# A written order for the last routing group of a mixture-of-experts layer, woven with pieces of expert work already known

## The chip, the cores and the metric

The kernel runs on one core of one Trainium2 chip. The core has a matrix engine (PE, with its weight load shown apart as PEld), a vector engine (DVE), a scalar engine (ACT), GpSimd (POOL) and SyncE (SP). Each executes its own instructions in the order in which they stand; they meet through semaphores. Transfers are issued from the queues of SP, ACT and POOL. The metric is the device time of one execution in microseconds. Lines such as L1087 are lines of the kernel before.

## The reference

The program computes four layers over 2708 rows of 256 values; only layer 1 is touched. It normalizes the rows, adds a graph product, normalizes again, and sends every row through one of eight experts:

```python
# graph part
A = adj + I;  d = 1/sqrt(A.sum(1));  A = A * d[:, None] * d[None, :]
x = x + relu(A @ (layernorm(x) @ W) + b)
# expert part: one expert for each row, all experts share the hidden layer
xf = layernorm(x)
H = gelu(xf @ W1 + b1)                    # 256 -> 1024
probs = softmax(H @ Wg + bg)              # 8 experts
assign = argmax(probs)
out = sum over e of where(assign == e, probs[:, e] * (H @ Wd[e] + bd[e]), 0)
x = x + out
```

## The kernel before

The 2708 rows are 22 tiles of 128, the last with 20 rows. Layer 1 works in three groups (`GROUPS1`): tiles 0 to 7, 8 to 15 and 16 to 21. For each group the graph sums are made by a loop over all blocks of the adjacency (L1174), into four banks `acc2`. When a group's sums are complete, `grow` on DVE takes them out of the banks and adds them to `x` (L1125, L1127): these are the sums' exits.

Then `send1` routes the group. `stats` makes means and variances and takes the reciprocal root by a Newton iteration on DVE. For each pair of tiles `norm_to` (L187) normalizes on DVE, `turn_to` transposes on PE (L203) and copies on ACT (L204); `hidden` makes the eight slices of the hidden layer on PE (L357) with a Gelu on ACT (L359); sixteen gate products (L1070), a copy on ACT (L1073) and a folding product (L1077) give the logits, to which DVE adds the bias (L1078). The hidden rows are turned by DVE's block transposes into `hrow`, of which there are two buffers (L1087), and stored to `hid` in the main memory, four transfers for a tile (L1093, L1096 for the last tile). In the first two groups GpSimd issues these stores; in the last one ACT does. After the last pair come a softmax (L327 to L334, its exponential needs another table on ACT, L135), the choice of the best expert, and `route`, which gives each row its place in its expert's list (L384, L386 and small operations on DVE). GpSimd scatters the rows' names and weights to these places, one transfer for each tile (`taken`, L492). `blocks` turns the experts' counts into a table that says for each block of 128 list places which expert it has and where its names lie.

`Units` does the experts' work in such blocks. For a block GpSimd gathers the names (L506) and then the rows of the hidden layer (L643, three buffers `hs`), SP fetches the expert's weights (`wb`, L1010, three buffers of 1152 KB), PE turns the rows by eight transposes (L654), ACT copies them (L655), PE makes sixteen products (L693), DVE adds the bias and applies the weight (L694, L695, two buffers `ys`), and GpSimd scatters the output rows to `given` (L492). Nine blocks are certain once two of the three groups are routed: they hold only rows of the first two groups. The next fifteen need the routing of the last group. A conditional region for still more blocks follows, and then layer 2.

What stands in a program is not the order on an engine: a planner with estimated costs orders the instructions of each engine by readiness and by their place in the program. Edges between two instructions (`after`, `add_manual_dep`) restrict it. In the kernel before, `send1` of the last group comes first in the program and the nine certain blocks with the fifteen others after it, in `work1.run(hc, items, beside)`, and the planner weaves them. The weaving shown in the timeline is its choice. `beside` is called by `run` for each block, and for block 13 (`NA + 4`) it adds work for layer 2: two loads of rows and one of weights by GpSimd, eight operations on DVE (L259, L260) and a centring product (L235, L237).

## Time and profile before

| what | us |
|---|---|
| median of three runs | 1936.62 (1930.79 to 1938.07) |
| the profiled execution | 1935.32 |
| its span, first to last instruction | 1933.6 |
| PE busy in the span | 1827.5 |
| last group's sums end, first exit begins | 930.1 |
| first transposes of the last group's pairs | 950.45 |
| last logit of the last group | 990.35 |
| softmax's sum | 996.32 |
| end of PE's work on certain blocks and the centring | 1012.2 |
| first transposes of an uncertain block | 1028.51 |
| last product of an uncertain block | 1101.25 |
| layer 2 begins to load | 1108.4 |

Times from 930 on are microseconds after the start of the span. A line of a stage's busy time gives the window, its length, the busy time and count of each engine, the mean granted clock of PE as a share of full speed, the share of the transfer engines that was busy and their rate. A line of the timeline gives start, duration, engine, line, operation, operands and count; in brackets stands how long the engine was idle before it and what ended that. SPq, ACTq and POOLq are issues of transfers.

### The profile page before, as it was taken

Reading aid. Unit: us, or ns where it says so; the run is one execution under the profiler, and the core shown is the slowest. Engines: PE = TensorE matmul, PEld = TensorE weight load, DVE = VectorE, ACT = ScalarE, POOL = GpSimd, SP = SyncE. Lnnn points to the kernel's source line nnn. Section 1 sums busy time; section 2 is a strip of 40 time slices with the busy share of each in tenths; the row PEclk is TensorE's granted clock in tenths of the full one; section 3 lists DMA queues with packets and bytes.
Section 4 is the critical chain, followed back from the end, with each engine's and each line's share of the span. In section 5 each row is a group of like instructions: output and inputs, shape, how many; then the busy total and the mean of one; then the engine's idle time right before and its main releaser. Section 6 shows DMA issues by size and latency. Waiting matters only on the chain.

```text
span 1933.6 us, 25684 instructions
## 1 busy us (share of the span) xinstructions
PE 1827.5 (95%) x9453; PEld 1327.0 (69%) x9453; DVE 1092.7 (57%) x2439; ACT 642.1 (33%) x1461; POOL 344.5 (18%) x405
## 2 busy tenths in 40 slices
PE   7999989999998999999796799999899999999998
PEld 6888778888887888888676678888557732232344
DVE  7776862444333524444441175555354398999897
ACT  7868732222223303122231142223232552031131
POOL 1005263333321002314336300000000000000000
PEclk9999989999998999999898999999899999999999
DMA  8435476887764454535777620000101000000000
GB/s 274 138 114 155 120 273 243 342 311 282 301 254 133 144 151 118 149 106 131 222 243 262 264 75 1 1 1 1 44 1 33 17 1 23 23 12 28 20 20 15
DMA packets 90141, 243.94 MB, mean 126 GB/s; under 512 B 18159, under 2 KB 44823, under 8 KB 80792
## 3 DMA queue, kind: packets, MB, share of 16 engines
q1 hardware_dynamic: 70048, 197.09, 30.9%
q0 software_dynamic: 16960, 42.42, 6.9%
q10 hardware_dynamic: 3000, 2.70, 0.5%
q8 instruction: 78, 1.28, 0.3%
q14 instruction: 55, 0.45, 0.1%
HBM read 216.29 MB, written 28.71 MB: 127 GB/s over the span
## 4 chain that ended last, share of the span: by engine, by line
PE 73%; DMA 12%; DVE 6%; issue 5%; ACT 2%; POOL 2%; SPq 0%; POOLq 0%; DVEq 0%; ACTq 0%
PE num L1803 10%; PE ps_acc L1382 9%; PE acc L1174 8%; PE ps_tmp L357 7%; PE acc L893 7%; PE den L1813 6%; PE ps_acc L591 5%; PE yacc L601 4%; PE ps_tmp L250 4%; DMA given<-ys,xs 4%; PE ps_acc L1566 3%; PE yacc L693 2%; DMA hs<-hid,names 2%; DMA given<-ys,names 1%; PE ps_tmp L203 1%
## 5 line engine op out<-in xcount | busy, mean ns | idle before, releaser
L1773 DVE SCALAR_TENSOR_TENSOR e<-arena,G,mask 128x1024 f32<-128x1024 f32 (+1 forms) x264 | 287.0, 1149 | 13.6 <-PE den L1813 13.6
L1803 PE MATMUL num<-e,wh 128*64 128x512 f32 (+4 forms) x1056 | 215.8, 551 | 0.0
L1382 PE MATMUL ps_acc<-hh,e 128*128 128x257 f32 x882 | 199.2, 382 | 1.7 <-ACT o L1327 1.7
L893 PE MATMUL acc<-msg,wt 128*128 128x256 f32 x882 | 198.5, 382 | 2.0 <-DVE wt L851 1.2
L1174 PE MATMUL acc<-sup,adrow 128*128 128x256 f32 x882 | 198.6, 382 | 1.8 <-DVE adrow L1146 1.8
L893 PEld LDWEIGHTS acc<-msg,wt 128*128 128x128 f32 x882 | 165.6, 191 | 28.0 <-DVE wt L851 2.1
L1174 PEld LDWEIGHTS acc<-sup,adrow 128*128 128x128 f32 x882 | 165.1, 190 | 28.7 <-issue 5.2
L1382 PEld LDWEIGHTS ps_acc<-hh,e 128*128 128x128 f32 x882 | 163.7, 190 | 29.2 <-ACT o L1327 4.3
L591 PE MATMUL ps_acc<-xTs,wa 128*128 128x256 f32 (+1 forms) x768 | 170.6, 375 | 1.0 <-DVE xTs L564 0.8
L593 ACT ACTIVATE hTs<-ps_acc,wa 128x256 f32<-128x256 f32 (+1 forms) x192 | 88.6, 464 | 244.4 <-PE yacc L601 165.6
L601 PE MATMUL yacc<-wb,hTs 128*128 128x256 f32 x736 | 167.4, 380 | 1.9 <-DVE ys L603 1.9
L591 PEld LDWEIGHTS ps_acc<-xTs,wa 128*128 128x128 f32 x768 | 137.6, 191 | 27.3 <-DVE xTs L564 3.8
L1803 PEld LDWEIGHTS num<-e,wh 128*64 128x64 f32 (+1 forms) x1056 | 66.5, 136 | 127.3 <-issue 106.5
L601 PEld LDWEIGHTS yacc<-wb,hTs 128*128 128x128 f32 x736 | 137.6, 190 | 20.2 <-DVE ys L603 2.7
L1376 DVE SCALAR_TENSOR_TENSOR e<-Rb,G,mask 128x640 f32<-128x640 f32 (+2 forms) x110 | 85.1, 775 | 93.1 <-PE ps_acc L1382 93.0
L1813 PE MATMUL den<-e,wh 128*32 128x512 f32 (+4 forms) x1056 | 118.0, 548 | 0.0
L204 ACT COPY xT<-ps_tmp 128x256 f32<-128x256 f32 x98 | 33.6, 364 | 242.5 <-PE ps_tmp L203 217.2
L1143 DVE TENSOR_SCALAR mask<-adrow 128x1024 uint8<-128x1024 f32 (+1 forms) x66 | 41.7, 631 | 124.2 <-DMA adrow<-in_adjT 124.0
L693 PE MATMUL yacc<-wb,hTs 128*128 128x256 f32 x384 | 90.6, 387 | 0.3 <-DMA wb<-in_L_ffn_Wdp 0.3
L851 DVE SCALAR_TENSOR_TENSOR wt<-adrow,wt 128x640 f32<-128x640 f32 (+3 forms) x67 | 71.1, 1063 | 30.6 <-ACT wt L141 30.3
L1813 PEld LDWEIGHTS den<-e,wh 128*32 128x32 f32 (+1 forms) x1056 | 30.2, 108 | 77.9 <-issue 73.8
L492 POOL DMA_INDIRECT given<-ys,xs x46 | 65.9, 1432 | 83.7 <-DVE ys L604 77.9
(452 smaller groups left out, 2570.8 us busy)
## 6 DMA issues: line engine op xcount, KB each, us to landing
adhalf<-in_adjT SPq DMA_DIRECT2D x42, 677.0 KB
wb<-in_L_ffn_W2p SPq DMA_DIRECT2D x24, 1152.0 KB
wb<-in_L_ffn_Wdp SPq DMA_DIRECT2D x24, 1152.0 KB
wa<-in_L_ffn_W1b SPq DMA_DIRECT2D x24, 1028.0 KB
adrow<-in_adjT SPq DMA_DIRECT2D x42, 512.0 KB
adrow<-in_adjT SPq DMA_DIRECT2D x42, 320.0 KB
adrow<-in_adjT SPq DMA_DIRECT2D x21, 576.0 KB
adrow<-in_adjT SPq DMA_DIRECT2D x21, 448.0 KB
```

What stands on the lines that cost most here:

```text
L357: te.matmul(p[:, :w], lhsT=w1[:, c, f * P : (f + 1) * P], rhs=xnT[:, c, c0 : c0 + w], start=(c == 0), stop=(c == DC - 1))
L591: te.matmul(p[:, f % 2, : m * P], lhsT=w1[:, c, f * P : (f + 1) * P], rhs=xT[:, c, : m * P], start=(c == 0), stop=(c == DC - 1))
L593: s.activation(hT[:, f, : m * P], p[:, f % 2, : m * P], AF.Gelu, bias=bias[:, f : f + 1])
L601: te.matmul(q[:, k, :], lhsT=hT[:, f, k * P : (k + 1) * P], rhs=w2[:, f, :], start=(f == 0), stop=(f == HC - 1))
L693: te.matmul(q, lhsT=hT[:, f, :], rhs=w2[:, f, :], start=(f == 0), stop=(f == HC - 1))
L893: te.matmul(p[:q, n - pair[0], :], lhsT=wt[:, k : k + q], rhs=msg[:r, j, :], start=(j == 0 and n == pair[0]), stop=(j == FULL - 1 and n == ...
L1174: te.matmul(p[:q, n - pair[0], :], lhsT=ad[:, k : k + q], rhs=sup[:r, j, :], start=(j == 0 and n == pair[0]), stop=(j == FULL - 1 and n == ...
L1376: v.scalar_tensor_tensor(e[:r, :w], Rb[:r, c0 : c0 + w], G[:r, j, :], mask[:r, j, c0 : c0 + w], op0=ALU.max, op1=ALU.mult)
L1382: te.matmul(p[:, : D + 1], lhsT=e[:, k : k + q], rhs=hh[:, j, :], start=(j == 0), stop=False)
L1773: v.scalar_tensor_tensor(e[:, :w], slow[:, m % 2, k, :w], G[:, j, 2 * pair + k, :], mask[:, j, c0 : c0 + w], op0=ALU.max, op1=ALU.mult)
L1803: te.matmul(num[k * DK : (k + 1) * DK, hf, :q], lhsT=wh[some, j, 2 * pair + k, :DK], rhs=e[some, h0 - c0 : h0 - c0 + q], start=(j == 0), s ...
L1813: te.matmul(den[z : z + Q, :q], lhsT=wh[some, i, 2 * pair + k, DK : DK + 1] .to_broadcast([some.stop - some.start, Q]), rhs=e[some, h0 - c ...
```

## The change

Only the last group of layer 1 is treated differently. `Units.run` becomes `add` (put blocks on the list) and `pieces`, a generator that gives control back after each block's transposes and after each block's output. `send1` is cut into parts (`normed`, `first_products`, `gate_products`, `add_up`, `keep`). For the last group it takes the generator as `fill` and calls for a piece at written places: the transposes of blocks 0, 1, 2 and 3 and the products and outputs of blocks 0 and 1 lie between the parts of the three pairs. The sums' exits are now bank by bank, each followed by the statistics of its own two tiles, and the first two norms follow the first statistics. At the end `in_order` chains every instruction made since the exits began on PE, DVE and ACT, transfers issued by ACT among them, to the one before it on its engine; it is the helper that stood further down, moved up. The last pair's hidden rows are stored after this and by GpSimd; the first two pairs' by ACT as before. The operations of `beside` on DVE get an edge behind the last output made so far, that of block 12.

```diff
+        def pieces(self, pool, during=None):
+
             turned = self.turn(pool, self.rows[0][1])
+            yield
             n = 0
             while self.rows:
                 w2, hT = self.ahead.pop(0), turned
...
                 if self.rows:
                     turned = self.turn(pool, self.rows[0][1])
+                    yield
                 y = pool.tile([P, D], F32, name="ys", bufs=2)
...
-                v.tensor_scalar(y, y, m[:, 1:2], None, op0=ALU.mult)
+                i = v.tensor_scalar(y, y, m[:, 1:2], None, op0=ALU.mult)
+                self.last = i.ins.name
                 scatter(self.given, m[:, 0:1].bitcast(I32), y, self.given.shape[0] - 1, self.ok)
+                yield
...
-                queue = s if tiles is GROUPS1[-1] else g
+            def keep(own, hT, queue):
...
+            if fill is None:
+                st = stats(tiles)
+                for own in pairs:
+                    hT = first_products(own, normed(own, (0, st)))
+                    add_up(own, gate_products(own, hT))
+                    keep(own, hT, g)
+            else:
+                start, st, made = begun
+                next(fill)
+                xT = normed(pairs[0], None, made)
+                for n, own in enumerate(pairs):
+                    hT = first_products(own, xT)
+                    next(fill)
+                    lT = gate_products(own, hT)
+                    if n + 1 < len(pairs):
+                        xT = normed(pairs[n + 1], (2 * (n + 1), st[n + 1]))
+                        next(fill)
+                    add_up(own, lT)
+                    if n + 1 < len(pairs):
+                        keep(own, hT, s)
+                in_order(start, (mybir.EngineType.PE, mybir.EngineType.DVE,
+                                 mybir.EngineType.Activation))
+                keep(own, hT, g)
             pin()
...
+        def beside(b):
+            if b == NA + 4:
+                first = len(nc.cur_bb.bb.instructions)
+                left.append(blocks_left(too_many, MOST))
...
+                centre(w_l2)
+                for i in nc.cur_bb.bb.instructions[first:]:
+                    if i.engine == mybir.EngineType.DVE:
+                        tc.add_manual_dep(i, work1.last, mybir.DependencyInfo(
+                            mybir.DependencyClass.NoSync, mybir.DependencyReason.DATA),
+                            reason="order")
...
+            else:
+                begun = len(nc.cur_bb.bb.instructions), [], []
+                for n in range(0, len(tiles), 2):
+                    grown(n // 2)
+                    begun[1].append(stats(tiles[n : n + 2]))
+                    if n == 0:
+                        for k in range(2):
+                            begun[2].append(work.tile([P, D], F32, name="xn"))
+                            norm_to(begun[2][k], tiles[k], k, begun[1][0])
                 sums.close()
                 gnn.close()
                 psum_pool(l1, 3, 3)
...
                 work1.more()
+                between = work1.pieces(hc, lambda b: beside(b))
+                send1(tiles, begun, between)
+                break
...
-        work1.run(hc, items, beside)
+        work1.add(items)
+        for _ in between:
+            pass
         work1.run_rest(hc, more, left[0])
```

The helper, moved up unchanged:

```python
    def in_order(first, engines):

        was = {}
        for i in nc.cur_bb.bb.instructions[first:]:
            if i.engine in engines:
                if i.engine in was:
                    tc.add_manual_dep(i, was[i.engine], ...)   # order only, no semaphore
                was[i.engine] = i.name
```

## The prediction

> **What bounds the kernel now.** I read the page's shares first, then the busy time by stage around the change, then the timeline of that stretch engine by engine, then the waits. The whole program sits on the matrix engine:
>
> ```profile
> span 1933.6 us, 25684 instructions
> PE 1827.5 (95%) x9453; PEld 1327.0 (69%) x9453; DVE 1092.7 (57%) x2439; ACT 642.1 (33%) x1461; POOL 344.5 (18%) x405
> ```
>
> PE is busy 95% of the span, so time can only come from PE's holes or from half clock. Busy time by stage (PE, PEld, DVE, ACT, POOL, then PEclk, DMA share, GB/s) shows one hole inside the stretch that the change rewrites:
>
> ```profile
> 931.00:943.00 12.00, 3.37 (x18) 2.43 (x16) 9.13 (x40) 2.24 (x4) 5.47 (x6) 0.73 0.94 345
> 943.00:990.00 47.00, 46.46 (x276) 38.78 (x276) 13.14 (x32) 18.80 (x42) 12.79 (x13) 0.96 0.74 250
> 1012.00:1028.50 16.50, 0.16 (x1) 0.02 (x1) 2.77 (x8) 0.00 (x0) 10.67 (x13) 0.59 0.88 244
> 1028.50:1101.30 72.80, 68.46 (x360) 58.89 (x360) 12.50 (x34) 17.48 (x31) 39.41 (x39) 0.98 0.80 295
> ```
>
> From 1012 to 1028.5 PE does nothing: the nine certain blocks are used up and the first uncertain block waits for its hidden rows. The timeline shows why that comes late (start, length, engine, line, operands, idle before):
>
> ```profile
> 949.65 0.42 DVE L694 TENSOR_TENSOR ys<-yacc,wb 128x256 f32<-128x256 f32 x1 [9.35 <-PE yacc L693]
> 949.99 1.87 DVE L187 TENSOR_SCALAR xn<-x,mv,rs_y 128x256 f32<-128x256 f32 x5
> ...
> 960.89 3.84 ACTq L1093 DMA_DIRECT2D hid<-hrow  x8
> ...
> 971.86 0.71 DVE L1087 STREAM_TRANSPOSE hrow<-hT 128x512 f32<-128x512 f32 x1 [3.58 <-DMA hid<-hrow]
> ...
> 990.20 0.15 DVE L1078 TENSOR_TENSOR lg<-ps_tmp,L_ffn_bg 20x8 f32<-20x8 f32 x1 [0.51 <-PE ps_tmp L1077]
> ...
> 991.27 2.46 ACTq L1096 DMA_DIRECT2D hid<-hrow  x4
> ...
> 993.76 1.28 ACT L135 ACT_TABLE_LOAD   x1 [4.72 <-DMA hid<-hrow]
> ...
> 996.32 0.20 DVE L332 TENSOR_REDUCE s_sm<-s_e 128x6 f32<-128x48 f32 x1
> ...
> 1019.17 0.42 DVE L694 TENSOR_TENSOR ys<-yacc,wb 128x256 f32<-128x256 f32 x1 [9.57 <-DMA given<-ys,names]
> ...
> 1028.51 1.94 PE L654 MATMUL ps_acc<-ident,hs 128*128 128x128 f32 x8 [16.35 <-DMA hs<-hid,names]
> ```
>
> Statistics are done at 940.3, but the first block's output (L694) stands ahead of the norms on DVE, so pair work starts at 950. The last logit is there at 990.35; then ACT is still issuing stores until 993.7, loads the exponential's table, and the softmax's sum runs at 996.32. From there to the first uncertain block 32.1 us pass: routing, six scatters, the names gather, the rows gather. That chain, not PE, sets 1028.5. I take it unchanged.
>
> **The change, part by part.** I lay out the new order with durations of this execution. One block is T (eight transposes, 0.87) and P (sixteen products, 3.46); these and PE's other lengths come from the pieces of the chain of waits between 950 and 992.
>
> *Start.* DVE's first sums' exit is at 930.08 as before. Two tiles' exits (0.88 + 0.75), four statistics operations (1.1), variance and eleven Newton operations spaced 0.2 as at 939.3 to 940.3 (2.35), two norms (0.75): the first norm is ready at 935.5 instead of 950.4. Eight operations on the next layer's weights (L259, L260, 0.4 each, 3.2 in sum), which lay among the statistics, go behind block 12's output. The other two pairs' exits and statistics follow on DVE until 945.3, beside the first pair's products; cover is thin, for pair two's norms (to 946.1) are wanted at 946.2.
>
> *Pair one.* PE transposes 0.9 and two copies on ACT, products from 936.9 for 6.9; the Gelu table (1.28) is nearly hidden by the three free banks, 0.3 left: 944.1. T of block 1, 945.0; gate 1.2, 946.2; pair two's transposes 947.1; P of block 0, 950.55; folding 0.4, 950.95.
>
> *Pair two: the price of writing the order.* DVE now does block 0's output (0.8), logits (0.35) and only then four transposes (2.6): 954.4. Before they ran as soon as half of the Gelus were done. Behind them ACT issues eight stores at 0.48 each (the row of 3.84), from 953.15 to 957.0, and the next Gelu stands behind those. PE fills its three banks (2.6) by 953.55, then stands for 4.0. After 4.9 us of idleness at 934.5 the next eight transposes took 1.94 instead of 1.04, and half clock lasted some 3.5 us after the restart at 1028.5 (granted clock 0.50 from 1027 to 1031, 0.86 from 1031 to 1035), so a stall costs another 1.75, bounds 0 and 1.8; I take 1.75. Products end 963.6; T 0.87, gate 1.2, transposes 0.7, P 3.46, folding 0.4: 970.3.
>
> *Pair three.* Three banks 1.6 (the 148-column products, 4.03 for eight), 971.8. DVE's output, logits and transposes end 973.7, ACT's stores 976.2, the stall is 4.9, and with half clock the products end 981.1. T 0.9, gate 0.9, copy and folding 0.8: last logit at 984.1, 6.2 before the old one. In sum the start gains 14.9 and the order gives back 8.7.
>
> *Last rows' stores.* ACT loses eight issues (989.0 to 993.7), so the table load can begin at once; from last logit to the softmax's sum were 6.0, and could be 1.0. Against this, pair three's DVE transposes wait until pair two's stores have landed (9.0 us from issue by the row at 971.86), that is until about 985, and they may stand ahead of the softmax. Bounds: gain 5.0, or 0 if an output of block 2 (PE 3.46) stands ahead too. I take 3.8, nearer the first: at 996.3 one output (0.8) stood ahead of that sum, and the transposes' wait for the stores adds about 1. GpSimd gains eight issues of 0.553 (its own row for the earlier groups), 4.4, between 979 and 990, before the six scatters can start near 992; queued behind them are rows gathers with two blocks of slack. Cost zero while routing covers it; 4.4 if it doesn't.
>
> The Trainium skill's page DMA: Bandwidth & Descriptors, section Issuing engine by pattern, speaks against this part: plain stores belong on the hardware-generated queues, which it calls generally faster. By that rule the 4.6 us on ACT would be the cheap place and this term no gain, 1929.6 in place of the sum below; the rows say that the place matters more than the issue, since nothing short of a table load waits behind ACT's.
>
> *Sum for the chain.* 6.2 + 3.8 = 10.0: the first uncertain block at 1018.5. PE's supply until then: at 983.9 seven P and five T remain, 28.6, and 2.0 of routing products, to 1014.5. So PE stands 4 us in place of 16.35, and the chain still sets the time.
>
> *After.* The centring of next layer's weights (PE 1.03, DVE 4) falls among the uncertain blocks, where PE waits for rows anyway; 0 to 3, taken 0.5. DMA share was 0.88 in the hole and would carry the same bytes in less time; the first five uncertain blocks ran at 4.22 each and the later ten at 5.17, so losing that head start could cost up to 4.8; taken 0, since their rows are asked for after the names in either order. SP's weight fetches wait for block outputs, as now. Gain 9.5 us.
>
> **The sum.** The profiled execution took 1935.3 (span 1933.6 and 1.7 around it), 1.3 under the median 1936.6. 1935.3 - 9.5 = 1925.8. Measurements of this kernel tell about 0.5%, 9.7 us.
>
> **Rivals.**
> - *No stalls.* If the planner's free instructions or quicker stores close both stalls, and half clock stays away (8.9 + 3.5 back), PE's supply is the limit: the hole's 16.35 and the 1.8 of half clock at its end bound the gain at 18. Time 1917 to 1922, 1920 likeliest. For it: ACT's stores for tile one can overlap the second's transposes. Against: ACT's queue is in order and the Gelus are written behind.
> - *Given back.* Names and rows land later (rows took 3.2 to 13.8, median 6.9; 6.4 in this chain), or the head start of 4.8 goes: 10 less 4 to 10, 1929 to 1936, 1932 likeliest. For it: DMA share 0.94 and 0.88 at both ends.
> - *Slower: DVE behind the scatters of outputs.* There are two output buffers. At 1019.17 DVE had stood 9.57 for a scatter that GpSimd could not issue earlier, harmless there. Now seven outputs run while softmax, routing and block tables are queued on the same DVE, and GpSimd has stores, scatters and gathers for all of 979 to 1003. One such wait ahead of them eats the 10.0; two make 1935.3 + 9.1 = 1944. It decides from 10 us of waits on. Against: those outputs come 4.3 us apart, and a scatter landed in 7.1.
> - *It does nothing:* the edges fix the order on PE, DVE and ACT, so this can be no more than a part of the second rival.
>
> **Chances.** Forecast 0.45 (1922 to 1929, its own range), no stalls 0.25, given back 0.18, slower 0.12. Faster by over 0.5% (under 1926.9): 0.27 of the forecast and all of the first rival, 0.52. Slower: 0.10. The rest, 0.38, is same. The range leaves out the slower rival and little else: 1917 to 1937.
>
> **What the changed profile would show.** First pair's transposes near 936; on ACT eight stores and then a Gelu, with PE idle 4 to 5 us near 954 and 972 and a clock under 1.0 after each; last folding near 984; the exponential's table load directly after; GpSimd's stores before the scatters; PE's hole before the first uncertain block at about 4 us, its T near 1018. Wrong, if the last logit comes after 988, if DVE's outputs wait for scatters before the block table, or if the fifteen uncertain blocks take more than 76 us in place of 72.8.

## The result, and the profile after

The changed kernel takes 1940.3 us (median of 11 runs, 1935.74 to 1945.54) where the kernel before, run beside it, takes 1937.99 us (1928.09 to 1941.96): a ratio of 1.0017, 95% interval 1.0004 to 1.0029. 1925.8 was forecast. Measured again later the ratio was 1.0029 (1.0014 to 1.0043). So the change costs 0.2 to 0.3%, 3 to 6 us, less than the 0.5% below which the forecast speaks of the same time.

In what follows TensorE is the PE of the views, VectorE is DVE, ScalarE is ACT. Line numbers in views of the kernel after are lines of that kernel (L1129 and L1132 are the stores, L653 the rows gather, L664 the turns, that is a block's eight transposes, L713 its sixteen products).

First the page's shares for the kernel after: TensorE is still busy 95% of the span, which is 2.0 us longer.

```profile
span 1935.6 us, 25698 instructions
PE 1833.2 (95%) x9453; PEld 1329.0 (69%) x9453; DVE 1098.6 (57%) x2465; ACT 641.8 (33%) x1461; POOL 351.6 (18%) x413
```

The busy time by stage, kernel after (PE, PEld, DVE, ACT, POOL, granted clock, share and rate of transfers):

```profile
931.00:943.00 12.00, 7.83 (x39) 6.36 (x40) 10.76 (x49) 5.42 (x11) 4.34 (x5) 1.00 0.96 385
943.00:990.00 47.00, 38.23 (x229) 31.79 (x228) 14.51 (x50) 15.09 (x36) 11.87 (x15) 0.89 0.60 189
...
1005.00:1023.50 18.50, 7.49 (x34) 6.19 (x34) 2.33 (x6) 2.25 (x4) 12.33 (x13) 0.82 0.77 266
1023.50:1105.80 82.30, 73.49 (x380) 62.45 (x380) 17.76 (x49) 17.39 (x31) 45.82 (x48) 0.98 0.82 298
```

The hole ahead of the first uncertain block (1012 to 1028.5 before) is broken up, but little of it is filled: from the end of the graph sums to the first uncertain block's turn TensorE is idle for 24.5 us in place of 27.3, and from 1005 to 1023.5 for 11 of 18.5. The stretch from there to the last product takes 82 us in place of 72.8, with 380 matmuls in place of 360; and from 943 to 990 transfers run at 189 GB/s in place of 250. The timeline, kernel after, where PE waits and what it waits for:

```profile
934.38 1.06 PE L664 MATMUL ps_acc<-ident,hs 128*128 128x128 f32 x8 [3.63 <-DMA hs<-hid,names]
...
936.72 2.86 PE L367 MATMUL ps_tmp<-xT,L_ffn_W 128*128 128x256 f32 x12 [0.63 <-ACT xT L214]
...
953.16 4.65 ACTq L1129 DMA_DIRECT2D hid<-hrow  x8
...
958.44 6.97 PE L367 MATMUL ps_tmp<-xT,L_ffn_W 128*128 128x256 f32 x20 [4.14 <-ACT hT L369]
...
974.75 5.42 ACTq L1129 DMA_DIRECT2D hid<-hrow  x8
...
980.71 4.27 PE L367 MATMUL ps_tmp<-xT,L_ffn_W 128*128 128x148 f32 x20 [3.77 <-ACT hT L369]
...
986.91 1.28 ACT L135 ACT_TABLE_LOAD   x1
...
987.90 0.15 DVE L1114 TENSOR_TENSOR lg<-ps_tmp,L_ffn_bg 20x8 f32<-20x8 f32 x1 [0.35 <-PE ps_tmp L1113]
...
988.97 0.20 DVE L342 TENSOR_REDUCE s_sm<-s_e 128x6 f32<-128x48 f32 x1 [0.44 <-ACT s_e L141]
...
1011.47 1.94 PE L664 MATMUL ps_acc<-ident,hs 128*128 128x128 f32 x8 [6.63 <-DMA hs<-hid,names]
...
1023.69 1.06 PE L664 MATMUL ps_acc<-ident,hs 128*128 128x128 f32 x8 [3.83 <-DMA hs<-hid,names]
1024.59 5.30 PE L713 MATMUL yacc<-wb,hTs 128*128 128x256 f32 x16
```

Up to the softmax's sum this is the predicted picture, 7.35 us ahead of before: the pairs start near 936, two stalls stand behind ScalarE's stores, the table load comes at once. Block 7, a certain block, is then late at 1011.47, and the first uncertain block at 1023.69 is only 4.8 us ahead. The sixteen products at 1024.59 are those of block 8, the last certain one: `pieces` writes a block's products behind the next block's turn, and with block 7 late they fall behind the first uncertain turn. In the kernel before they were done by 1011.3. GpSimd's timeline says why block 7 is late (the rows gathers of blocks 6, 7, 8 and 9 are the four lines of `hs`):

```profile
986.13 1.04 POOL L653 DMA_INDIRECT hs<-hid,names  x1 [7.06 <-PE ps_acc L664]
987.60 2.26 POOL L1129 DMA_DIRECT2D hid<-hrow  x4 [0.43 <-DVE lg L1114]
989.85 2.06 POOL L1132 DMA_DIRECT2D hid<-hrow  x4
995.24 1.08 POOL L502 DMA_INDIRECT taken<-names,r_ix  x1 [3.32 <-issue]
...
1002.93 0.91 POOL L502 DMA_INDIRECT taken<-names,r_ix  x1 [0.31 <-issue]
1004.15 1.00 POOL L502 DMA_INDIRECT given<-ys,names  x1 [0.30 <-DMA taken<-names,r_ix]
1005.46 1.04 POOL L516 DMA_INDIRECT names<-taken,b_ix  x1 [0.30 <-issue]
1006.81 1.00 POOL L653 DMA_INDIRECT hs<-hid,names  x1 [0.31 <-issue]
...
1010.79 1.00 POOL L653 DMA_INDIRECT hs<-hid,names  x1 [0.31 <-issue]
...
1015.36 0.99 POOL L653 DMA_INDIRECT hs<-hid,names  x1 [0.90 <-issue]
```

The buffer of block 7's rows was free when block 4 had been turned, at 988.1. Its gather is queued behind the eight stores, the six scatters, an output and a gather of names, and goes at 1006.81; in the kernel before it went at 976.82, ahead of all of them. The stores cost little here (GpSimd stands 3.3 us after them), the order does.

### The profile page after: what moved, and what is told of

Its sections match the earlier page's. It is cut to its first block, busy times and chain, and to the rows that moved or that the text cites. A ratio compares the mean times of both kernels' runs of the same rounds, so it can differ in the third digit from the quotient of the medians.

```text
span 1935.6 us, 25698 instructions
## 1 busy us (share of the span) xinstructions
PE 1833.2 (95%) x9453; PEld 1329.0 (69%) x9453; DVE 1098.6 (57%) x2465; ACT 641.8 (33%) x1461; POOL 351.6 (18%) x413
## 4 chain that ended last, share of the span: by engine, by line
PE 39%; DMA 4%; DVE 3%; issue 2%; ACT 2%; POOL 1%; ACTq 0%; POOLq 0%; DVEq 0%; SPq 0%
PE num L1876 10%; PE ps_acc L1455 9%; PE den L1886 6%; PE ps_tmp L367 5%; PE ps_acc L1639 3%; PE ps_tmp L260 2%; DMA given<-ys,names 1%; DMA names<-taken,b_ix 1%; PE ps_acc L260 1%; PE ps_tmp L213 1%; PE yacc L713 1%; DVE e L1846 1%; DMA hs<-hid,names 0%; DMA taken<-names,r_ix 0%; DVE e L1449 0%
## 5 line engine op out<-in xcount | busy, mean ns | idle before, releaser
L611 PE MATMUL yacc<-wb,hTs 128*128 128x256 f32 x736 | 167.3, 379 | 2.4 <-DVE ys L613 2.4
L1876 PEld LDWEIGHTS num<-e,wh 128*64 128x64 f32 (+1 forms) x1056 | 66.5, 136 | 127.3 <-issue 105.6
L713 PE MATMUL yacc<-wb,hTs 128*128 128x256 f32 x384 | 89.8, 388 | 2.9 <-DMA wb<-in_L_ffn_Wdp 2.2
L367 PE MATMUL ps_tmp<-xT,L_ffn_W 128*128 128x256 f32 (+1 forms) x352 | 80.6, 386 | 8.7 <-ACT hT L369 8.1
```

The costliest lines, as they stand in the source:

```text
L367: te.matmul(p[:, :w], lhsT=w1[:, c, f * P : (f + 1) * P], rhs=xnT[:, c, c0 : c0 + w], start=(c == 0), stop=(c == DC - 1))
L611: te.matmul(q[:, k, :], lhsT=hT[:, f, k * P : (k + 1) * P], rhs=w2[:, f, :], start=(f == 0), stop=(f == HC - 1))
L713: te.matmul(q, lhsT=hT[:, f, :], rhs=w2[:, f, :], start=(f == 0), stop=(f == HC - 1))
L1876: te.matmul(num[k * DK : (k + 1) * DK, hf, :q], lhsT=wh[some, j, 2 * pair + k, :DK], rhs=e[some, h0 - c0 : h0 - c0 + q], start=(j == 0), s ...
```

## Experiments

Three theories. **A:** GpSimd's in-order queue sets the pace after the softmax. **B:** next-layer work placed between the uncertain blocks holds VectorE and through it the outputs. B' widens this from the layer-2 weight, which the change's edges put there, to layer 3's loads and score columns, which the planner brings along. **C:** the transfers' rate bounds the second half, whatever the order.

To compare runs whose stage begins at different times, I count from the end of the last graph sum on TensorE (931.34 in the kernel before, 930.74 after). "MB" is what was moved in the first 100 us of that count, the window's rate times its length; "GB/s" is the rate of the next 60 us.

| kernel | DVE edges | softmax sum | MB | GB/s | last product | layer 2 loads | ratio to before |
|---|---|---|---|---|---|---|---|
| before | no | 65.0 | 24.5 | 332 | 169.9 | 177.1 | 1 |
| before, again | no | 66.5 | 24.4 | 327 | 169.8 | 176.4 | 1.0004 (0.9990 to 1.0018) |
| after | yes | 58.2 | 22.7 | 337 | 175.0 | 179.4 | 1.0017 (1.0004 to 1.0029) |
| after, again | yes | 66.4 | 21.1 | 295 | 185.2 | 189.5 | 1.0029 (1.0014 to 1.0043) |
| e1_free | no | 59.6 | 22.5 | 349 | 171.7 | 176.0 | 0.9997 (0.9983 to 1.0011) |
| e2_act | yes | 65.5 | 22.6 | 276 | 185.4 | 191.8 | 1.0044 (1.0029 to 1.0059) |
| e3_rows | yes | 61.5 | 21.7 | 289 | 185.2 | 189.5 | 1.0033 (1.0019 to 1.0047) |
| e4_pool | yes | 48.7 | 24.1 | 302 | 175.8 | 180.4 | 0.9995 (0.9980 to 1.0010) |
| e5_hold | no | 60.8 | 22.4 | 353 | 169.5 | 178.6 | 1.0031 (1.0018 to 1.0043) |
| e6_before_hold | no | 62.7 | 23.7 | 346 | 165.9 | 174.8 | 1.0013 (0.9994 to 1.0031) |
| e7_sp | no | 49.1 | 23.0 | 356 | 167.3 | 176.2 | 0.9992 (0.9977 to 1.0006) |
| e8_half | yes | 56.2 | 18.2 | 248 | 165.0 | 169.3 | 0.9932 (0.9909 to 0.9955) |
| e9_before_half | no | 61.3 | 18.8 | 240 | 159.8 | 166.5 | 0.9934 (0.9917 to 0.9951) |
| e10_four | yes | 61.4 | 22.3 | 320 | 181.1 | 185.5 | 1.0007 (0.9991 to 1.0023) |
| e11_before_four | no | 63.4 | 25.6 | 324 | 169.8 | 176.9 | 0.9990 (0.9976 to 1.0004) |
| e12_best | no | 54.7 | 22.8 | 356 | 174.6 | 181.0 | 0.9979 (0.9966 to 0.9991) |
| e13_dve | no | 48.8 | 22.4 | 360 | 170.4 | 176.7 | 0.9989 (0.9974 to 1.0004) |
| e14_act | no | 49.2 | 23.1 | 356 | 169.8 | 176.1 | 1.0010 (0.9993 to 1.0026) |
| e15_best_late | no | 49.1 | 23.6 | 362 | 170.4 | 177.2 | 0.9987 (0.9978 to 0.9997) |
| e16_late | yes | 60.3 | 22.6 | 313 | 177.9 | 182.5 | 1.0029 (1.0018 to 1.0040) |

The stage columns are of one profiled execution each. They can be ones off the median: the profiled "after, again" took 1946.89 where the median is 1941.32. Ratios rest on all runs.

### Each part alone: the edges, the stores, the queue

**e1_free** takes the edges out that put the layer-2 weight's VectorE work behind block 12's output.

```diff
-                for i in nc.cur_bb.bb.instructions[first:]:
-                    if i.engine == mybir.EngineType.DVE:
-                        tc.add_manual_dep(i, work1.last, ..., reason="order")
```

> The changed kernel without the edge that holds the eight operations on layer 2's weights behind block 12's output. Theory B (the deferred operations cost the uncertain blocks): DVE's 8.1 us behind a load and PE's 2.5 us around the centring leave the stretch of the fifteen uncertain blocks, which falls from 82 to 76 us or less; time 5 to 7 us under the changed kernel, near 1934. Theory A (GpSimd's queue, which gathers the rows of blocks 7 and 8 only behind the six scatters, sets the pace): at most 2 us less. Theory C (the transfers' rate, 298 GB/s in this stretch against 295 before, bounds the stage whatever the order): within 2 us.

0.9997: the loss is gone, the gain is not there. (Its interval, 0.9983 to 1.0011, overlaps that of 1.0017, not that of 1.0029.) The stretch of the uncertain blocks takes 79.0 us in place of 82.1: it holds the same 380 matmuls, busy for 73.9 us, and TensorE is idle in it for 5.1 us in place of 8.6. Layer 2 begins 3.4 us earlier than in the kernel after. Work is still brought in between them; VectorE waits, in the kernel after and then in e1_free:

```profile
1063.11 0.43 DVE L269 TENSOR_TENSOR o<-w_l,L_gnn_a_l 128x256 f32<-128x256 f32 x1 [8.10 <-DMA L_gnn_a_l<-in_L_gnn_a_l]
```

```profile
1060.58 0.76 DVE L269 TENSOR_TENSOR o<-w_l,L_gnn_a_r 128x256 f32<-128x256 f32 x2 [11.31 <-DMA w_l<-in_L_gnn_WT]
```

Both are layer 3's score columns, which the planner takes up where their loads are listed; in the kernel before the same wait (6.53 us at 1027.18) fell into the hole.

**e2_act** gives the last pair's stores back to ScalarE.

```diff
-                keep(own, hT, g)
+                keep(own, hT, s)
```

> The changed kernel with the last pair's rows stored by ACT, as before the change. ACT's eight issues stand again ahead of the exponential: softmax's sum 4 to 5 us later, near 993, and the six scatters begin near 999 in place of 995. Theory A: first uncertain block 3 to 4 us later, time 2 to 4 us more. Theory B and C: time within 2 us of the changed kernel, because what follows takes up the difference.

The table load comes at 1002.86, behind the pair's eight issues (998.71 to 1002.82), and the softmax's sum at 65.5 after the graph sums in place of 58.2. 1.0044 against 1.0017 and 1.0029: GpSimd's stores seem worth the place that they free on ScalarE, 3 to 5 us, but the second interval overlaps.

**e3_rows** asks for six more pieces of the blocks ahead of the scatters in the text.

```diff
+            if fill is not None:
+                for _ in range(6):
+                    next(fill)
             for i, t in enumerate(tiles):
                 r = rows(t)
                 scatter(taken[1], ix[:r, i, :], names[:r, i, :], N - 1, "taken1")
```

> The changed kernel with the pieces up to block 6's transposes written ahead of the last group's six scatters, so that GpSimd gathers the rows of blocks 7 and 8 before it scatters. Theory A: PE's wait of 6.6 us before block 7 goes, the certain blocks end near 1009 in place of 1020, the first uncertain block starts near 1016 in place of 1023.7, time 5 to 7 us under the changed kernel, near 1934. Theory B: the start moves but the deferred operations still fall among the uncertain blocks, so half of it, 3 us. Theory C: the uncertain blocks take the gain back by a longer stretch, time within 2 us.

Rows of blocks 7 and 8 now go at 1009.14 and 1014.05 ahead of the scatters, but GpSimd first has to wait for the outputs of the blocks before them, the scatters move to 1015.39 to 1021.94 and the hole comes back, 8.48 us ahead of the first uncertain block. 1.0033: no better than the kernel after. Neither order of one queue is right; what is put first delays the other.

**e4_pool** has GpSimd issue all the group's stores.

```diff
-                        keep(own, hT, s)
+                        keep(own, hT, g)
```

> The changed kernel with all three pairs' rows stored by GpSimd, so that no Gelu stands behind ACT's stores. PE's two stalls of 4.1 and 3.8 us and the half clock after them go, last logit 8 to 10 us earlier, near 979. Theory A: GpSimd's rows gathers come behind sixteen more issues of 0.55, but its queue was empty for much of 953 to 986, so the scatters begin near 987 and the first uncertain block 5 us earlier; time 3 to 5 us less. Theory B: the gain of 5 stays, minus nothing; 3 to 5 us less as well. Theory C: within 2 us.

The two stalls on ScalarE are gone (one of 0.66 us is left) and the softmax's sum is 9.5 us earlier than in the kernel after, at 48.7. Of this nothing arrives at the last product, 175.8 in place of 175.0: the rows of block 6 are gathered at 1010.12, behind all the rest, and PE stands 15.93 us. The ratio 0.9995 is below the kernel after's all the same.

### Holding the next layers' work; stores by SyncE

**e5_hold** is e1_free with order edges that put layer 2's and 3's loads on GpSimd behind the last scatter, and layer 3's score columns behind the last output. **e6_before_hold** is the same on the kernel before. **e7_sp** is e5_hold with all stores by SyncE; the last two lines are its alone, and the later `keep(own, hT, g)` changes in the same way.

```diff
+        held_behind = scattered["given1"][-1].name, work1.last
...
+    def held(first):
+        for i in nc.cur_bb.bb.instructions[first:]:
+            if i.engine in (mybir.EngineType.Pool, mybir.EngineType.DVE):
+                tc.add_manual_dep(i, held_behind[i.engine == mybir.EngineType.DVE], ..., reason="order")
...
+        mark = len(nc.cur_bb.bb.instructions)
         wr = mat(tp, "L2_ffn_Wr", E)
...
+        held(mark)
...
-                        keep(own, hT, s)
+                        keep(own, hT, nc.sync)
```

> The kernel after, without the order edges that put the layer-2 weight's vector work behind the last certain block (the edit of the run without them), and with new order edges: the next layers' GpSimd loads behind the last scatter of the uncertain blocks, layer 3's score columns and their loads behind the last uncertain block's vector work. Theory B' (work of the next layers, hoisted between the uncertain blocks, costs GpSimd about 5 us of issue and VectorE a wait of 8 to 11 us): the uncertain blocks take 73 to 75 us in place of 79.0 to 82.1, ratio 0.996 to 0.998. Theory A (the in-order queue of gathers and scatters sets the pace by itself): 77 to 79 us, ratio 0.999 to 1.001. Theory C (the rate of transfers): no change, 79 us and more.

> The kernel before with the same order edges on the next layers' loads and score columns. In the kernel before this work lies in the hole of 20 us ahead of the uncertain blocks, where it costs little. Theory B': nothing is gained here, ratio 0.999 to 1.002, and the uncertain blocks take 72 to 74 us as now. If holding the work is worth as much here as it is in the kernel after, B' is no reason for the loss between the two.

> The same as the kernel after with the held work, and all 24 stores of the last group's rows issued by SyncE, none by ScalarE or GpSimd. If ScalarE's stores make the two stalls of 4.1 and 3.8 us with their half-clock stretches, both are gone, the last logit comes 8 to 10 us earlier against the stage's start, the scatters of names follow. Theory A: the row gathers of blocks 6 and 7 then still stand behind the six scatters, the hole moves forward but stays, the uncertain blocks take 77 to 79 us: ratio 0.997 to 1.000. Theory B': 73 to 75 us and the whole gain of the start: ratio 0.990 to 0.995. Theory C: the ratio stays at 0.999 to 1.002.

In the stage B' fits: e5_hold's uncertain blocks take 75.2 us in place of 79.0 (the two profiles of the kernel before differ by 2.3 us in this stretch). In the whole it doesn't: 1.0031. What was held is paid at layer 2's start, 9.0 us from the last product to the loads in place of 4.4, and behind it: from the loads to the end of the span the three held kernels take 827.8 to 829.6 us, the kernel before 825.2. The chain of waits of e7_sp shows the price, one of four small loads ahead of the next stage:

```profile
1108.25 0.98 POOL given L502
1109.23 0.24 POOL L_ffn_Wr L127
1109.48 0.50 issue
1109.98 0.33 POOL L_ffn_br L121
...
1110.55 5.03 DMA b<-in_L_ffn_b
...
1115.98 2.66 DMA mine<-given
```

e6_before_hold gains 4 us at the last product, has 2.3 of it left at the loads and loses that behind them (1.0013). e7_sp is the surprise: softmax's sum 16 us earlier than before, first uncertain block 80.9 in place of 97.2, and the last product only 2.6 us earlier. The fifteen blocks seem to stretch to 86.4 us, which would speak for C. TensorE's and SyncE's timelines of e7_sp show something else:

```profile
1020.72 0.44 PE L664 MATMUL ps_acc<-ident,hs 128*128 128x128 f32 x1 [19.14 <-DMA hs<-hid,names]
1020.96 12.15 PE L713 MATMUL yacc<-wb,hTs 128*128 128x256 f32 x48
1032.95 0.93 PE L664 MATMUL ps_acc<-ident,hs 128*128 128x128 f32 x7
```

```profile
979.24 14.83 SPq L1129 DMA_DIRECT2D hid<-hrow  x12
999.26 1.41 SPq L1132 DMA_DIRECT2D hid<-hrow  x4
1001.83 40.89 SPq L1032 DMA_DIRECT2D wb<-in_L_ffn_Wdp  x8
```

TensorE stood 19.14 us for one transpose of the first uncertain block, and the 48 products of three certain blocks were queued behind that transpose. With those of a fourth, 64 of the 304 products in the 86.4 us are certain work, and TensorE is busy for 82.6 of them; from 1032.95, the rest of the turn, to the last product are 74.2 us, much as in the kernel before. SyncE, in turn, issued the next weights only at 1001.83, behind sixteen stores. In e13_dve below, with the same hole, three such fetches went from 996.63 on; transfers ran at 347 and 362 GB/s from 1000 to 1010, 3.5 MB or three blocks' weights, and at 80 GB/s from 1010 to 1015, and the 48 products began at 1015.44. So e7_sp is no evidence for C: what the earlier softmax brought went into a hole in which certain work stood behind one transpose. The same hole is in e12_best (12.49 us, 32 products behind it), e13_dve (19.21, 48), e14_act (20.56, 48) and e15_best_late (18.08, 32). No run puts these products ahead of that transpose.

### Half the bytes

**e8_half** and **e9_before_half** load half of each expert's second weights in these blocks and use it twice; the other half is left out of the result.

```diff
-            wb = wbs["pool"].tile([P, 2048 + D], F32, name="wb", bufs=3)
-            i = nc.sync.dma_start(wb, a["L1_ffn_Wdp"][bass.ds(e, 1)].rearrange("e p n -> p (e n)"))
+            wb = wbs["pool"].tile([P, 1024 + D], F32, name="wb", bufs=3)
+            i = nc.sync.dma_start(wb, a["L1_ffn_Wdp"][bass.ds(e, 1), :, 1024:].rearrange("e p n -> p (e n)"))
...
-                    te.matmul(q, lhsT=hT[:, f, :], rhs=w2[:, f, :], ...)
-                v.tensor_tensor(y, q, w2[:, HC, :], ALU.add)
+                    te.matmul(q, lhsT=hT[:, f, :], rhs=w2[:, f % 4, :], ...)
+                v.tensor_tensor(y, q, w2[:, 4, :], ALU.add)
```

> The kernel after, with only half of each expert's second weights loaded in layer 1's single blocks (0.66 MB in place of 1.18 MB a block) and the same half used twice, so half of these weights is left out of the computation. TensorE's work and every instruction stay as they are. Theory C (the transfers' rate bounds the uncertain blocks): they take 70 to 73 us in place of 82.1, by TensorE's own busy time of 73.5; ratio 0.993 to 0.996. Theories A and B' (GpSimd's queue, hoisted work): at least 79 us, ratio 0.999 to 1.002, since no wait on the weights is on the path.

> The kernel before with half of each expert's second weights loaded in layer 1's single blocks and the same half used twice (half of these weights is left out of the computation). The same edit took the kernel after to 1935.79 us (0.9932 of the kernel before). Theory C (the kernel after loses because two blocks' weights and rows are moved later, into a stretch in which the transfers run at their limit): with half the bytes the kernel before gains less than the kernel after did, 3 to 7 us, ratio 0.9960 to 0.9985, so that among the halved kernels the change is a gain. Theory A (GpSimd's queue alone makes the loss): the halving gives both kernels the same or nothing in the difference, and this one ends 2 to 4 us ahead of the halved kernel after, ratio 0.989 to 0.993.

The two halved kernels measure the same, 0.9932 and 0.9934 of the kernel before: 13 us less for the kernel before, and 16 to 19 for the kernel after, counted from its 1.0017 or 1.0029. In each the last product comes 10 us earlier; in the kernel after 3.2 of these are there by the first uncertain block, in the kernel before 6.8. TensorE waited for a weight only twice in this stretch of the kernel after, 2.2 us in sum, so it is not the waits on weights that go. The windows of 100 and 60 us after the graph sums, the kernel before and then e9_before_half, show the room made:

```profile
931.34:1031.34 100.00, 72.74 (x412) 61.23 (x413) 38.96 (x141) 26.75 (x56) 40.16 (x44) 0.87 0.76 245
1031.34:1091.34 60.00, 56.39 (x306) 48.91 (x305) 9.51 (x24) 13.96 (x26) 35.76 (x36) 0.99 0.90 332
```

```profile
940.88:1040.88 100.00, 78.88 (x450) 66.91 (x450) 39.78 (x143) 27.94 (x59) 44.95 (x48) 0.90 0.64 188
1040.88:1100.88 60.00, 58.30 (x315) 51.02 (x313) 10.33 (x27) 15.08 (x27) 32.80 (x33) 1.00 0.70 240
```

So the bytes count in both kernels. My finer claim, that with half of them the change would be a gain, did not come true: the two are equal, with intervals of about 4 us either way, and 0.9934 lies just outside the range named for A (0.989 to 0.993) and farther from that for C (0.9960 to 0.9985). The halved kernel after still has the edges, and PE there waits 4.02 us for the layer-2 weight's score columns (`PE L245` at 1059.16).

### A fourth buffer, and the fastest version

**e10_four** and **e11_before_four** have four buffers for the second weights; **e12_best** adds to e10_four no edges and all stores by SyncE.

```diff
-            hT = pool.tile([P, HC, P], F32, name="hTs", bufs=3)
+            hT = pool.tile([P, HC, P], F32, name="hTs", bufs=2)
...
-            while weights and self.todo and len(self.ahead) < 2:
+            while weights and self.todo and len(self.ahead) < 3:
...
-            wb = wbs["pool"].tile([P, 2048 + D], F32, name="wb", bufs=3)
+            wb = wbs["pool"].tile([P, 2048 + D], F32, name="wb", bufs=4)
```

> The kernel after with four buffers in place of three for the second weights (three blocks fetched ahead in place of two; the space comes from the turned rows, two buffers in place of three). Theory C: a further 1.2 MB is moved in the early stretch, where transfers use 0.47 to 0.72 of their time, and is missing from the full stretch at about 340 GB/s: 3 to 4 us gained, ratio 0.9990 to 1.0005 in place of 1.0017. Theory A: TensorE waits for rows, not for weights, so nothing changes: ratio 1.001 to 1.003. If two buffers for the turned rows cost something it shows as waits of TensorE's turns on ScalarE.

> The kernel before with the same four buffers. Its transfers use 0.71 to 0.74 of their time in the early stretch, and TensorE's blocks are ahead there, so less is to be had: theory C 1 to 3 us, ratio 0.9985 to 0.9995. Theory A: 1.000.

> The kernel after with four buffers, without the order edges on the layer-2 weight's vector work, and with all 24 stores of the last group's rows issued by SyncE; nothing held. From the runs so far: no edges gives 3.4 us at the start of layer 2, SyncE's stores take away the two stalls (softmax sum 9 us earlier against the stage's start) but only 2 to 3 us of that reached the end, as the transfers were full. Theory C: with the fourth buffer 3 to 4 us more, in all 6 to 9 us under the kernel before, ratio 0.995 to 0.997. Theory A: 2 to 4 us, ratio 0.998 to 0.999.

The fourth buffer moved 25.6 MB early in the kernel before in place of 24.5, and no more in the kernel after (22.3 in place of 22.7): there SyncE's fetches wait for outputs (68.6 us in 8 waits between 930 and 1050), since the blocks themselves are late. The ratios 1.0007 and 0.9990 don't part from 1.0017 and 1. e12_best is faster than the kernel before, 0.9979; the interval ends at 0.9991. Its profile does not show where: the last product and layer 2's loads come later than before, 174.6 and 181.0. In the eight profiles of that chip the graph sums end between 939.79 and 945.02, so one trace can't place 4 us. The ratio lies in what A had named (0.998 to 0.999, rounded), not in C's 0.995 to 0.997.

### Only VectorE held, loads on another queue, and the unchanged kernels again

> The kernel before, unchanged, profiled on the chip of the two next experiments. Every theory: ratio 1.000 within its interval; against the end of the stage's graph sums the softmax sum at about 65 us, the last product at 170 us, layer 2's loads at 177 us. Where these move by more than 2 us between two chips, differences of 2 us between single traces say nothing.

> The kernel after, unchanged, profiled on the same chip. If the loss is a property of the change: ratio 1.001 to 1.003 again, the softmax sum at about 58 us after the graph sums, the last product at 175 us, layer 2's loads at 179 us, and the uncertain blocks at 80 to 83 us.

The kernel before repeats within 1.5 us in the stage times of the table. The kernel after does not: 66.4 in place of 58.2 at the softmax's sum, 185.2 at the last product, in an execution 5.6 us over its median. Its first turn, in the profile of the kernel after again (timeline), stands 9.28 us:

```profile
930.41 1.02 POOL L653 DMA_INDIRECT hs<-hid,names  x1 [0.16 <-issue]
930.65 2.12 SPq L1032 DMA_DIRECT2D wb<-in_L_ffn_Wdp  x3
...
939.79 1.94 PE L664 MATMUL ps_acc<-ident,hs 128*128 128x128 f32 x8 [9.28 <-DMA hs<-hid,names]
```

**e13_dve** is e7_sp with only VectorE's score columns held; **e14_act** also has seven of the loads issued by ScalarE (`s.dma_start` in place of `g.dma_start`).

```diff
-            if i.engine in (mybir.EngineType.Pool, mybir.EngineType.DVE):
-                tc.add_manual_dep(i, held_behind[i.engine == mybir.EngineType.DVE], ...)
+            if i.engine == mybir.EngineType.DVE:
+                tc.add_manual_dep(i, work1.last, ...)
```

> The kernel after without its order edges on the layer-2 weight's vector work, all 24 stores issued by SyncE, and only layer 3's score columns (VectorE) held behind the last uncertain block; layer 2's and 3's loads stay where the planner puts them on GpSimd. Theory B' (hoisted work): the 5 us that the held loads cost at the start of layer 2 are saved, and VectorE waits for no load between the blocks: layer 2 begins 171 to 174 us after the graph sums, ratio 0.994 to 0.997. Theory A (GpSimd's queue): the loads are back between the gathers, so what is saved at layer 2's start is lost among the blocks: ratio 0.998 to 1.000. Theory C (transfers): same as the run with SyncE's stores and everything held, 0.999, less the part at layer 2's start: 0.996 to 0.998.

> The same, with seven of the loads (router weight and bias, two bias tables, two norm rows, layer 3's weight) issued by ScalarE in place of GpSimd. Theory A: 5 us of issue less in GpSimd's queue, so 3 to 5 us faster than the run with only VectorE held. Theories B' and C: the same time within 1.5 us.

In e13_dve the stalls, the edges and the wait for layer 3 are all gone, the softmax's sum is 16 to 18 us earlier than in the kernel before, and layer 2's loads come at 176.7, as before (176.4, 177.1). Its windows of 100 and 60 us:

```profile
934.33:1034.33 100.00, 73.49 (x413) 61.76 (x413) 40.08 (x161) 26.11 (x56) 40.32 (x45) 0.86 0.68 224
1034.33:1094.33 60.00, 55.62 (x303) 47.75 (x302) 10.11 (x26) 13.96 (x26) 35.12 (x35) 1.00 0.99 360
```

The transfers are full for the whole 60 us, and TensorE is busy for 55.62 of them. Its chain of waits runs through rows that need 10.60 and 8.83 us from issue to landing:

```profile
1043.50 10.60 DMA hs<-hid,names
...
1059.21 8.83 DMA hs<-hid,names
```

e14_act takes some 4.5 us of issue off GpSimd and has the same stage times (169.8, 176.1), so these loads are not what is left; whether the gathers behind scatters in GpSimd's queue are was not tested apart. Its ratio is 1.0010 (the interval overlaps e13_dve's). In its profile 6.7 us more pass behind layer 2's start: the busy times by window agree with e13_dve's for 800 us from there, and 5.6 of the 6.7 lie behind VectorE's last operation, 8.4 us from its end to the end of the span in place of 2.8. What makes the end longer was not found.

### Block 0's turns behind the first products

**e16_late** is the kernel after, **e15_best_late** is e12_best, with this:

```diff
-                next(fill)
                 xT = normed(pairs[0], None, made)
                 for n, own in enumerate(pairs):
                     hT = first_products(own, xT)
+                    if n == 0:
+                        next(fill)
                     next(fill)
```

> The fastest version so far (four buffers, no edges, SyncE's stores; 0.9979 of the kernel before) with block 0's turns behind the first products in place of ahead of the first transposes. If the wait for block 0's rows (9.4 us in its profile) is paid on the path: 3 to 6 us faster, ratio 0.994 to 0.997, first products about 5 us after the graph sums, the softmax sum at 46 to 50 us in place of 54.7. If the transfers in the second half set the end whatever comes before: 0.997 to 0.999.

> The kernel after with block 0's turns behind the first products, nothing else changed. If the wait for block 0's rows makes part of the loss: 1 to 4 us faster than the kernel after, ratio 0.999 to 1.001, and the softmax sum 57 to 59 us after the graph sums in every profile. If not: 1.0015 to 1.003.

The early wait is gone in both, and the time stays: 1.0029 for the kernel after with it, 0.9987 for the fast version, whose softmax's sum is 5.6 us earlier than e12_best's. The 9.3 us wait is real where it happens, and no part of the loss that these runs can measure.

## Why the prediction was wrong

*Start.* Right. The first two norms ran from 934.86 to 935.60 (the first was worked out for 935.5), block 1's turns began at 944.16 (944.1).

*The price of the written order.* Right in kind: stalls of 4.14 and 3.77 us (4.0 and 4.9), with slow products after each. But the last logit came at 987.90, 3.8 late. Eight stores took 4.65 and 5.42 us to issue in place of the 3.84 taken over from before (the kernel before has a second such row, 4.40 at 976.85, that I left aside); that is 2.4 of it, the rest I didn't resolve. With stores by another engine the stalls vanish but for 0.66 us (e4_pool, e7_sp), which shows their cause.

*Last rows' stores.* The softmax's sum came 1.07 us after the last logit, where I had taken 2.2. e2_act shows the part working. The Trainium skill (DMA: Bandwidth & Descriptors, Issuing engine by pattern) puts simple stores on Sync and calls the hardware-generated queues of Sync and ScalarE generally faster than GpSimd's. Here the last pair's stores measured 1.0044 on ScalarE and 1.0017 and 1.0029 on GpSimd, with overlapping intervals; the runs with SyncE (0.9979 to 1.0010, other edits among them) don't contradict the page's table.

*GpSimd "cost zero", "queued behind them are rows gathers with two blocks of slack".* This failed. The slack was counted against the stores alone; the gather of block 7 went 18.7 us after its buffer was free, behind stores, scatters and an output. Of 7.35 us at the softmax's sum 4.8 arrived at the first uncertain block. And the sum had TensorE done with the certain blocks at 1014.5, ahead of the first uncertain one; block 7 was turned at 1011.47, block 8 at 1016.64, and block 8's products came at 1024.59, behind the first uncertain turn.

*"After", and the sum's step from there.* This is the step that cost most. I let the fifteen uncertain blocks follow in 72.8 us wherever they begin, took 0.5 for the next layer's weights and 0 of 0 to 4.8 for the lost head start. They took 82.1 us, and the mark that I had named, 76, was passed. The rows of this stretch, 82.30 us after and 72.80 before, divide the difference: TensorE is busy for 5.0 us more, as 20 more matmuls lie there (block 8's sixteen products and the centring's four), and idle for 4.5 us more. This repeats: busy 73.5, 73.7 and 74.3 us and idle 8.6, 12.5 and 9.2 in after, after again and e16_late, busy 68.5 and 67.9 and idle 4.3 and 2.5 in the two profiles of the kernel before. What TensorE waited for in the kernel after (waits from 1020 to 1112; 3.8 of the 8.1 end at the first uncertain turn; in the kernel before rows 4.0 behind that turn, and weights 0.3):

```profile
PE ps_acc L664 <- DMA hs<-hid,names: 8.1, 6, 3.8
PE yacc L713 <- DMA wb<-in_L_ffn_Wdp: 2.2, 2, 1.5
PE ps_tmp L245 <- DVE w_l L270: 1.3, 1, 1.3
PE yacc L713 <- DVE ys L714: 0.7, 1, 0.7
```

- The edges on VectorE's layer-2 work: without them the ratio is 0.9997 in place of 1.0017 and 1.0029, so they cost some 4 to 6 us, and the idle time of the stretch is 5.1 us. The four lowest ratios on the changed kernel with whole weights (e12_best, e15_best_late, e13_dve, e7_sp) are all without them, but these also have SyncE's stores, and e4_pool, with the edges and without the stalls, has 0.9995. The two without them that lie above 1 lost their time at or behind layer 2's start (e5_hold, e14_act). How the edges cost it is not isolated: layer 3's columns are held up with and without them (8.1 and 11.3 us), and what TensorE waits for by itself is small (1.31 us in one profile, up to 6.32 in others).
- The transfers, argued and not shown to make the difference: between the end of the graph sums and the last product each kernel with whole weights moves 45 to 46 MB (rate times length of that window). When the gate is written first, blocks come late, SyncE's fetches wait for their buffers, and 1.8 MB less (24.5 against 22.7) has been moved after 100 us; at the 330 to 360 GB/s of the full stretch that would be 5 us. But TensorE's own waits for weights grew by only 1.9 us, and half the bytes took 10 us off the last product in both kernels.
- Seven kernels without the edges put the softmax's sum 4 to 18 us earlier than the kernel before, and their last product stays between 167 and 175 us, where before has 170. In five of them, those with SyncE's stores, 32 or 48 certain products stood behind one transpose of the first uncertain block while TensorE was idle for 12 to 21 us. How much of the earlier names would arrive without that is open, and so is whether the transfers would then be the limit.

My figure for the head start, "up to 4.8; taken 0, since their rows are asked for after the names in either order", looked at rows alone. The weights are the larger part (1152 KB a block), and they are fetched by block, not by name. No run shows whether the 4.8 us were lost. (The 32.1 us from the softmax's sum to the first uncertain block are 32.2 by the two rows; nothing hangs on it.)

*Rivals.* "Given back" is nearest in kind, at 1929 to 1936: rows landed later and part of the gain went. It had neither the edges nor the certain products behind the first uncertain turn. "Slower: DVE behind the scatters of outputs" did not occur ahead of the block table. Among the uncertain blocks VectorE did wait for scatters of outputs (36.2 us in 9 waits, 57.0 in 13 in e13_dve); a third output buffer was not tried, and whether it shortens the full stretch is open.

## What to carry to other kernels

Before a wait is shortened, count the work that will then lie behind it, engine by engine: here a certain block's products and the centring moved into the stretch that was to stay the same, and in the fastest versions 32 or 48 products of certain blocks stood behind one transpose that waited. When a step is moved ahead of others, note what the passed steps release: the last pair's stores and scatters, put first on GpSimd or SyncE, kept the rows and the weights of certain blocks waiting. And an order edge on one engine fixes more than its own instructions: what the planner lists behind them moves too, so it is worth one run with the edge alone taken out.

## What the runs showed of the hardware

- From the issue of block 0's rows gather to the turn that waited for it 4.2 to 5.4 us passed in the sixteen profiles in which GpSimd issued it 0.89 us or more ahead of SyncE's first weight fetch, and 9.4 us in the two in which it was 0.24 us (after, again) and 0.11 us (e12_best); there TensorE stood 9.28 and 9.41 us. What makes it so was not isolated.
- Transfers held 360 GB/s at a busy share of 0.99 for 60 us (e13_dve). In that stretch rows took 8.83 and 10.60 us from issue to landing.
